# One order of rows to the end of layer 0, own terms kept on the chip, one scratch tile for the dots

## The chip, the cores and the metric

The kernel runs on one core of one Trainium2 chip. A core has five engines that work side by side, each on its own list of instructions: TensorE (PE, matrix products and transposes, with weight loads shown apart as PEld), VectorE (DVE), ScalarE (ACT), GpSimd (POOL, here almost only the issue of indirect transfers) and SyncE (SP, which issues transfers). An engine goes through its list in order and waits at an instruction until the semaphores that it names have their values. Transfers run on 16 DMA engines. The metric is the time of one execution on the device, in microseconds (us).

## The reference

Two graph layers over 2048 nodes, for 8 batches of 256 channels. The adjacency matrix is symmetric, has ones on its diagonal and about 1 in 128 entries set, so a node has some 11 to 36 neighbours.

```python
# layer 0
h1, h2, h3 = inp @ W1, inp @ W2, inp @ W3
e = leaky_relu(einsum('bnd,bmd->bnm', h1, h2), 0.2)
attention = softmax(where(adj > 0, e, -1e12))
x = layernorm(x + relu(einsum('bnm,bmd->bnd', attention, h3)))
# layer 1, 4 heads of 64
q = x @ W
e = leaky_relu(e_src[:, i] + e_dst[:, j], 0.2)     # q times the halves of a, per head
attn = softmax(where(adj > 0, e, -9e15))
x = layernorm(x + elu(einsum('bijh,bjhd->bihd', attn, q)))
```

## The kernel before

The kernel doesn't form the 2048 x 2048 scores. It sorts the nodes by degree, lists each node's neighbours, and fetches for each node the rows of its neighbours. The nodes stand in 16 tiles of 128 by degree; a tile has so many slots as its largest degree asks (SLOTS, 11 to 36). The batches are taken in two halves h of four (HB), so a row is 4 x 256 numbers (HC = 1024). A unit is one tile of one half in one layer: 32 units of layer 0, then 32 of layer 1, each with 11 to 27 slots, 564 slots in a layer.

A unit of layer 0 goes like this. POOL gathers the rows of the unit's own nodes (own_rows) and, slot by slot, those of their neighbours into a ring of 16 chunks of two slots (chunk_job; L203 is the helper that records all gathers). The own rows are transposed on PE (turn, L501), copied to xT by ACT, multiplied by A = W1 W2^T (project, L509) and copied to g. For each slot DVE makes four dots, one per batch (dots, L727): a product of the neighbour's row with g, written to a scratch tile j in bf16 that nothing reads, and behind it the read of the accumulator into the score e. Softmax follows (L768 to L779 on DVE, the exponential on ACT, weights0 from L838 on DVE). ACT makes a diagonal matrix of each slot's weights and batch (dg, L937), and PE adds the weighted rows up (add_slot, L901).

These sums use TensorE in four quarters of 64 x 64: row half r and column half c. So a sum stands in *quarter order*: partition 64c + n holds node 64r + n, and the batch pair is c. ACT or DVE brings it into hs, still in quarter order. Then after0: PE transposes hs (turn_h), ACT copies it to hT, PE multiplies by W3 (project_h), DVE adds relu of it to the own rows xr and collects the statistics (residual, L1055 and L1058), ACT normalises in place (L487), SP stores the rows to x1s in DRAM (L1080), PE transposes again (turn_x) and makes q and the head terms (queries, L1096), ACT copies them to q_rows (L1435 is the line that runs every delayed step), SP writes the four query-side terms per batch to own_d in DRAM (L1112), and POOL scatters the rows of q to the table qg by node number (L211). All of this was in quarter order, so before0 first puts the own rows into quarter order with four transfers from SBUF to SBUF (L704; by ACT's queue for the first two units, SP's for the others), and q is scattered in two halves, with the index orderP.

A unit of layer 1 loads its own terms from own_d (before1, L1140) and x1s (sums1, L1291), gathers rows of qg, adds own and neighbour's terms (L1163), does softmax, weights the rows on DVE and ACT (L984, L974) and adds them up on PE (L901).

The order of DVE, ACT, PE and POOL is written out by the program. A counter steps once a slot (tick): due(n, step) records a step n ticks later, and the dots run ahead of the sums by the next part's slots plus 9. The list of every engine is thus fixed. A tile pool with bufs=n hands out n buffers in turn, and a writer waits for the last user of its buffer, on its own engine too. The own rows have one buffer, xo_rows; a unit's gather is recorded once the unit before is transposed (turned). The ring, xo_rows and q_rows:

```python
g_rows = held[0][:, : 2 * HC].rearrange("p (i c) -> p i c", i=2)
xo_rows, hs_rows = held[1][:, :HC], held[1][:, HC : 2 * HC]
```

Of the kernel before, what the change touches and what calls it, by code (L numbers as in the profile page):

```python
# [13 lines left out]
F32 = mybir.dt.float32  # L14
BF16 = mybir.dt.bfloat16
# [9 lines left out]
P = 128  # L25
# [114 lines left out]
def fast_path(  # L140
# [82 lines left out]
    own_d = [tc.dram_tile([N, HG], F32, name=f"own_{h}") for h in range(2)]  # L223
# [7 lines left out]
    q_rows = held[2][:, 2 * KC * C :][:, : 2 * (QW + 2 * H)].rearrange("p (r w) -> p r w", r=2)  # L231
# [43 lines left out]
    spare = q_rows.rearrange("p r w -> p (r w)")  # L275
# [126 lines left out]
    orderP = const.tile([P, NT, 2], I32, tag="orderP", name="orderP")  # L402
    half = const.tile([P, NT, 2], F32, tag="half", name="half")
    oidx = const.tile([P, 2, 2, NT, 2], I32, tag="oidx", name="oidx")
# [19 lines left out]
    nc.vector.scalar_tensor_tensor(orderP, orderR, 2.0, half, ALU.mult, ALU.add)  # L424
# [106 lines left out]
    class Unit:  # L531
        def __init__(self, layer, h, t):
# [22 lines left out]
            self.xo = None  # L555
            self.ready = self.turned = False
# [41 lines left out]
    def neighbours(t):  # L598
# [30 lines left out]
        far = sp.tile([P, 40], F32, tag="far", name=f"far_{t}", bufs=2)[:, :K]  # L629
# [62 lines left out]
    def own_rows(u):  # L692
        u.xo = xo_rows
        gather(u.xo, xg[u.h][:, :], order[:, u.t : u.t + 1])

    def before0(u):
        while u.xo is None:
            yield
        xo = u.xo
        u.xr = xrp.tile([P, 2, HW], F32, tag="xr", name=f"xr_{u.name}")  # L700
        queue = nc.scalar if u.index < 2 else nc.sync
        for r in range(2):
            for c in range(2):
                queue.dma_start(  # L704
                    u.xr[64 * c : 64 * c + 64, r, :], xo[64 * r : 64 * r + 64, ts(c, HW)]
                )
# [3 lines left out]
        turn(xo, f"x_{u.name}", xT)  # L710
        u.turned = True
# [12 lines left out]
    def dots(u, rows, others, into):  # L724
        for b in range(HB):
            jt = sp.tile([P, C], BF16, tag="j", name=f"j_{u.name}_{clock[0]}_{b}", bufs=4)
# [304 lines left out]
    def after0(u):  # L1031
# [12 lines left out]
        def turn_h():  # L1044
            u.hT = wide_tile(f"hT_{n}")
            turn(u.hs, f"h_{n}", u.hT)
# [7 lines left out]
        def residual(i, pp):  # L1054
            nc.vector.scalar_tensor_tensor(  # L1055
                u.y[:, ts(i, 512)], pp, 0.0, u.xr[:, i, :], ALU.max, ALU.add
# [32 lines left out]
        def queries(r):  # L1089
            if r == 0:  # L1090
                u.qrow = q_rows
            for j in range(2):
                i = 2 * r + j
                pq = ps_tile(f"ps_q_{n}_{i}")
                for k in range(KC):
                    nc.tensor.matmul(  # L1096
                        pq[:, : C + 2 * H],
# [8 lines left out]
            if r == 1:  # L1106
                due(3, own_terms)
# [678 lines left out]
```

## Time and profile before

| | |
|---|---|
| median of three runs (lowest, highest) | 2446.78 us (2442.81, 2447.77) |
| the profiled execution | 2466.09 us, its span 2464.2 us |
| PE, DVE, ACT, POOL busy in the span | 84%, 79%, 57%, 59% |
| transfers | 734.65 MB, 298 GB/s on average |
| first and last dot of layer 0 | 105.9 and 1382.7 us |
| mean of a dot's product, of its accumulator read | 421 ns, 82 ns |
| sums on PE, layer 0 and layer 1 | 712.1 us, 826.8 us |

A line of a group reads: line, engine, operation, what it writes <- what it reads, shapes, number; then busy time in all, mean of one in ns; then how long the engine sat idle just before these, and what ended most of that. The busy times of a stretch give for each engine the time it worked, with the number of its instructions; PEclk is the clock that TensorE was granted, as a share of its full one. In the order of time a row has the start, the length, the instruction and, in brackets, the idle time before it with its releaser.

### The profile page before, as it was taken

What the parts mean: (1) busy time and instruction counts of PE and PEld (TensorE: products, weight loads), DVE (VectorE), ACT (ScalarE), POOL (GpSimd) and SP (SyncE); (2) the same over time, 40 slices, a digit from 0 to 9 for tenths busy, and PEclk for the clock granted to TensorE, in tenths of its full rate; (3) what the DMA queues carried; (4) which work ended last, traced back from release to release, by engine and by line L of the source; (5) the groups of instructions that cost most, each with busy time, mean ns of one, the idle gap of its engine ahead of it and who ended that gap; (6) DMA issues with size and microseconds to landing.
All of it is one profiled execution on the core that took longest, in us unless ns stands there. A gap on an engine that the chain in (4) does not pass through costs nothing.

```text
span 2464.2 us, 50609 instructions
## 1 busy us (share of the span) xinstructions
PE 2060.1 (84%) x16234; PEld 1097.8 (45%) x16234; DVE 1951.7 (79%) x6799; ACT 1403.6 (57%) x4803; POOL 1442.0 (59%) x1411
## 2 busy tenths in 40 slices
PE   4168898898888999999999888888788888788885
PEld 2135565555655666666656543333233233232221
DVE  7487688888888786788788568888877787787887
ACT  6045676566576677766677656443564555443545
POOL 3354555555555556555565566666666666666662
PEclk9578899999899999999999998888898888988888
DMA  9987898888877889898888898988998898889981
GB/s 377 360 272 267 291 306 313 294 306 273 296 260 253 300 286 310 286 303 290 288 278 293 272 341 318 317 311 315 329 331 311 306 343 298 322 311 327 326 300 46
DMA packets 239649, 734.65 MB, mean 298 GB/s; under 512 B 53456, under 2 KB 62800, under 8 KB 236944
## 3 DMA queue, kind: packets, MB, share of 16 engines
q0 software_dynamic: 182784, 645.78, 75.3%
q1 hardware_dynamic: 54720, 83.39, 10.1%
q8 instruction: 132, 2.16, 0.3%
q10 hardware_dynamic: 1872, 2.16, 0.3%
q14 instruction: 141, 1.16, 0.1%
HBM read 674.46 MB, written 76.02 MB: 305 GB/s over the span
## 4 chain that ended last, share of the span: by engine, by line
PE 48%; DVE 14%; issue 14%; ACT 8%; DMA 5%; another core or an unknown queue 4%; POOL 3%; SPq 0%; ACTq 0%; POOLq 0%; DVEq 0%
PE acc L901 32%; DVE s L984 6%; PE ps_q L1096 5%; PE ps_p_h L509 4%; PE ps_p_g L509 3%; POOL s L203 3%; ACT s L974 2%; DVE j L727 2%; DMA s<-qg,idx 2%; PE ps_t_x L501 2%; ACT dg L937 2%; PE ps_t_h L501 1%; DMA edges<-adj 1%; DVE xr L1339 1%
## 5 line engine op out<-in xcount | busy, mean ns | idle before, releaser
L901 PE MATMUL acc<-s,ident 64*64 64x512 f32 x4496 | 826.8, 673 | 165.7 <-issue 128.2
L203 POOL DMA_INDIRECT s<-xg,idx x564 | 591.1, 1048 | 512.8 <-PE acc L901 271.3
L727 DVE CUSTOM_DVE_ANT_0 j<-s,held 128x256 bf16<-128x256 f32 x2248 | 799.2, 421 | 58.5 <-ACT held L718 24.5
L901 PE MATMUL acc<-s,dg 64*64 64x256 f32 x8992 | 712.1, 401 | 113.4 <-issue 69.1
L203 POOL DMA_INDIRECT s<-qg,idx x564 | 573.0, 1016 | 299.9 <-issue 150.8
L937 ACT ACTIVATE dg<-twice,e 128x64 f32<-128x64 f32 x2248 | 574.0, 340 | 99.1 <-remote 60.2
L901 PEld LDWEIGHTS acc<-s,ident 64*64 64x64 f32 x4496 | 291.3, 148 | 689.2 <-issue 612.8
L901 PEld LDWEIGHTS acc<-s,dg 64*64 64x64 f32 x8992 | 395.3, 138 | 383.5 <-issue 203.7
L984 DVE TENSOR_TENSOR s<-s,p 128x2048 f32<-128x2048 f32 (+1 forms) x246 | 542.9, 2210 | 0.1
L974 ACT ACTIVATE s<-s,e 128x64 f32<-128x64 f32 x1376 | 342.7, 335 | 69.9 <-DVE e L1239 37.5
L727 DVE DVE_READ_ACCUMULATOR2_ANT e<- 128x1 f32 x2248 | 184.6, 82 | 0.4 <-issue 0.3
L211 POOL DMA_INDIRECT out_dram<-o,oidx x128 | 130.1, 1016 | 72.2 <-ACT o L487 36.0
L1435 ACT ACTIVATE e<-e 128x40 f32<-128x40 f32 (+19 forms) x88 | 27.5, 312 | 216.8 <-DVE e L1219 108.7
L1096 PE MATMUL ps_q<-wqs,x1T 128*128 128x264 f32 x512 | 135.8, 405 | 6.1 <-issue 3.5
L509 PE MATMUL ps_p_g<-held,xT 128*128 128x256 f32 x512 | 129.3, 407 | 13.4 <-ACT xT L1435 11.5
L509 PE MATMUL ps_p_h<-held,hT 128*128 128x256 f32 x512 | 120.0, 386 | 0.6 <-issue 0.6
L509 PEld LDWEIGHTS ps_p_g<-held,xT 128*128 128x128 f32 x512 | 101.6, 204 | 40.5 <-issue 13.1
L1096 PEld LDWEIGHTS ps_q<-wqs,x1T 128*128 128x128 f32 x512 | 93.8, 193 | 46.8 <-issue 21.5
L1055 DVE SCALAR_TENSOR_TENSOR y<-ps_p_h,xr 128x512 f32<-128x512 f32 x64 | 44.0, 688 | 85.5 <-PE ps_p_h L509 52.6
L1435 ACT COPY held<-ps_q 128x264 f32<-128x264 f32 x128 | 46.3, 379 | 110.8 <-PE ps_q L1096 93.6
L509 PEld LDWEIGHTS ps_p_h<-held,hT 128*128 128x128 f32 x512 | 94.8, 190 | 26.6 <-issue 14.3
L1163 DVE TENSOR_TENSOR e<-s,own 128x32 f32<-128x32 f32 (+1 forms) x290 | 53.0, 187 | 66.9 <-DMA s<-qg,idx 55.0
(206 smaller groups left out, 1549.9 us busy)
## 6 DMA issues: line engine op xcount, KB each, us to landing
adj<-in_adj_dram SPq DMA_DIRECT2D x16, 1024.0 KB
x1s<-y SPq DMA_DIRECT2D x32, 512.0 KB
xr<-x1s SPq DMA_DIRECT2D x32, 512.0 KB
xr<-held SPq DMA_DIRECT2D x120, 128.0 KB
s<-xg,idx POOLq DMA_INDIRECT x564
s<-qg,idx POOLq DMA_INDIRECT x564
edges<-adj SPq DMA_DIRECT2D x16, 512.0 KB
xg<-in_x_dram SPq DMA_DIRECT2D x4, 2048.0 KB
```

The source lines that it names most:

```text
L203: nc.gpsimd.indirect_dma_start(out=dst, out_offset=None, in_=table, in_offset=AT(ap=index, axis=0), bounds_check=table.shape[0] - 1, oob_i ...
L211: ins = nc.gpsimd.indirect_dma_start(out=table, out_offset=AT(ap=index, axis=0), in_=src, in_offset=None)
L501: nc.tensor.transpose(pt[:, ts(j, P)], src[:, ts(4 * i + j, P)], ident)
L509: nc.tensor.matmul(pp[:, ts(j, C)], lhsT=srcT[:, ts((2 * i + j) * KC + k, P)], rhs=weight[:, k, :], start=(k == 0), stop=(k == KC - 1),)
L727: nc.vector.tensor_tensor_reduce(out=jt, in0=rows[:, ts(b, C)], in1=others(b), scale=1.0, scalar=0.0, op0=ALU.mult, op1=ALU.add, accum_out ...
L901: nc.tensor.matmul(out, lhsT=lhsT, rhs=rhs, start=(k == 0 and j == 0), stop=(k == K - 1 and (j == 1 or diag is None)), tile_position=(64 * ...
L937: nc.scalar.activation(diag[:, b, :], twice, AF.Copy, scale=u.p[i][:, b, k : k + 1])
L974: nc.scalar.activation(v[:, a, g, :], v[:, a, g, :], AF.Copy, scale=pv[:, a, g : g + 1])
L984: nc.vector.tensor_tensor(v, v, pv.unsqueeze(3).to_broadcast([P, n, H, D]), ALU.mult)
L1096: nc.tensor.matmul(pq[:, : C + 2 * H], lhsT=u.x1T[:, ts(i * KC + k, P)], rhs=w.sqs[:, k, j * H : j * H + CD + H], start=(k == 0), stop=(k ...
L1163: nc.vector.tensor_tensor(e[:, k : k + ns, :].rearrange("p s (b g) -> p s b g", b=HB), rows[:, :ns, :].rearrange("p s (b w) -> p s b w", b ...
L1435: heappop(events)[2]()
```

## The change

Rows of layer 0 are brought into node order where hs is transposed, and stay in it: the copy from the transposes to hT puts the columns of the quarters next to each other (by_node), so that the projection, the residual, the normalisation, x1s and q have a node per partition. The own rows are gathered straight into the buffers xr, of which there are five (four of the pool, and xo_rows for every fifth unit), and serve the transposes and the residual; the transfers of L704 go, and a unit's gather is recorded once the buffer of the unit five before is free. q is scattered as whole rows with the index order. The four query-side terms per batch are copied by ACT into owns, a tile in SBUF that layer 1 reads; own_d, its stores and its loads go, and queries uses one set of columns, 260 in place of 264. x1s is in node order now, and layer 1 brings it into quarter order with four transfers in place of one. The scratch tile j of the dots has one buffer in place of four, and far, a small tile of the lists, one in place of two.

```diff
@@ -220,7 +220,6 @@
     edges = tc.dram_tile([N, N], I16, name="edges")
     x1s = [tc.dram_tile([N, HC], F32, name=f"x1s_{h}") for h in range(2)]
     qg = [tc.dram_tile([N, 2 * QW], F32, name=f"qg_{h}") for h in range(2)]
-    own_d = [tc.dram_tile([N, HG], F32, name=f"own_{h}") for h in range(2)]
 
 
     nc.scalar.preload_act_table_set("natural_log_exp_and_others")
@@ -228,7 +227,7 @@
     setup.__enter__()
     held = [ring_tile(f"held_{i}") for i in range(MORE)]
     kept = held[2][:, : 2 * KC * C].rearrange("p (i k c) -> p i k c", i=2, k=KC)
-    q_rows = held[2][:, 2 * KC * C :][:, : 2 * (QW + 2 * H)].rearrange("p (r w) -> p r w", r=2)
+    q_rows = held[2][:, 2 * KC * C :][:, : 2 * QW + 4 * H]
     w = Weights(nc, const, wp, ps_tile, w1, w2, w3, wq, a, C, "", (kept[:, 0], kept[:, 1]))
     ident = w.ident
 
@@ -399,8 +398,8 @@
 
 
     orderR = const.tile([P, NT, 2], I32, tag="orderR", name="orderR")
-    orderP = const.tile([P, NT, 2], I32, tag="orderP", name="orderP")
     half = const.tile([P, NT, 2], F32, tag="half", name="half")
+    owns = const.tile([P, 2, NT, HG], F32, tag="owns", name="owns")
     oidx = const.tile([P, 2, 2, NT, 2], I32, tag="oidx", name="oidx")
     idx = const.tile([P, total], I32, tag="idx", name="idx")
     neg = const.tile([P, total], F32, tag="neg", name="neg")
@@ -421,7 +420,6 @@
                 tile_position=(64 * r, 64 * c),
             )
         nc.vector.tensor_copy(orderR[:, :, r], pr)
-    nc.vector.scalar_tensor_tensor(orderP, orderR, 2.0, half, ALU.mult, ALU.add)
     w.terms()
     setup.__exit__(None, None, None)
     ctx.enter_context(tc.manual_schedule(engines={mybir.EngineType.Pool}))
@@ -552,8 +550,8 @@
             self.ps = [None] * len(self.parts)
 
             self.m, self.s, self.diags = [], [], []
-            self.xo = None
-            self.ready = self.turned = False
+            self.xr = None
+            self.ready = False
 
 
     scored, tabled = [0], [0]
@@ -626,7 +624,7 @@
                 nc.vector.match_replace(some, m[:, ts(i, 8)], some, 0.0)
             yield
         nc.vector.tensor_scalar(neg[:, o : o + K], m[:, :K], 0.5, LOWEST, ALU.is_lt, ALU.mult)
-        far = sp.tile([P, 40], F32, tag="far", name=f"far_{t}", bufs=2)[:, :K]
+        far = sp.tile([P, 40], F32, tag="far", name=f"far_{t}", bufs=1)[:, :K]
         nc.vector.tensor_scalar(far, m[:, :K], 0.5, FAR, ALU.is_lt, ALU.mult)
         nc.vector.scalar_tensor_tensor(
             idx[:, o : o + K], m[:, :K], 1.0, far, ALU.subtract, ALU.add
@@ -690,25 +688,19 @@
         numbered_extras[0] = True
 
     def own_rows(u):
-        u.xo = xo_rows
-        gather(u.xo, xg[u.h][:, :], order[:, u.t : u.t + 1])
+        if u.index % 5 == 3:
+            u.xr = xo_rows
+        else:
+            u.xr = xrp.tile([P, HC], F32, tag="xr", name=f"xr_{u.name}")
+        gather(u.xr, xg[u.h][:, :], order[:, u.t : u.t + 1])
 
     def before0(u):
-        while u.xo is None:
+        while u.xr is None:
             yield
-        xo = u.xo
-        u.xr = xrp.tile([P, 2, HW], F32, tag="xr", name=f"xr_{u.name}")
-        queue = nc.scalar if u.index < 2 else nc.sync
-        for r in range(2):
-            for c in range(2):
-                queue.dma_start(
-                    u.xr[64 * c : 64 * c + 64, r, :], xo[64 * r : 64 * r + 64, ts(c, HW)]
-                )
         for _ in range(4):
             yield
         xT = wide_tile(f"xT_{u.name}")
-        turn(xo, f"x_{u.name}", xT)
-        u.turned = True
+        turn(u.xr, f"x_{u.name}", xT)
         for _ in range(4):
             yield
         while scored[0] < u.index - 1:
@@ -723,7 +715,7 @@
 
     def dots(u, rows, others, into):
         for b in range(HB):
-            jt = sp.tile([P, C], BF16, tag="j", name=f"j_{u.name}_{clock[0]}_{b}", bufs=4)
+            jt = sp.tile([P, C], BF16, tag="j", name=f"j_{u.name}_{clock[0]}_{b}", bufs=1)
             nc.vector.tensor_tensor_reduce(
                 out=jt,
                 in0=rows[:, ts(b, C)],
@@ -1043,7 +1035,14 @@
 
         def turn_h():
             u.hT = wide_tile(f"hT_{n}")
-            turn(u.hs, f"h_{n}", u.hT)
+            by_node = u.hT[:, :HC].rearrange("p (c j k r n) -> p j (k r) c n", c=2, j=2, k=KC, r=2)
+            for j in range(2):
+                pt = ps_tile(f"ps_t_h_{n}_{j}")
+                for k in range(KC):
+                    for r in range(2):
+                        o = r * HW + j * C + k * P
+                        nc.tensor.transpose(pt[:, ts(2 * k + r, P)], u.hs[:, o : o + P], ident)
+                due(2, nc.scalar.copy, by_node[:, j], pt.rearrange("p (a c n) -> p a c n", a=4, c=2))
 
         def project_h():
             u.y = wide_tile(f"y0_{n}")[:, :HC]
@@ -1053,7 +1052,7 @@
 
         def residual(i, pp):
             nc.vector.scalar_tensor_tensor(
-                u.y[:, ts(i, 512)], pp, 0.0, u.xr[:, i, :], ALU.max, ALU.add
+                u.y[:, ts(i, 512)], pp, 0.0, u.xr[:, ts(i, 512)], ALU.max, ALU.add
             )
             nc.vector.bn_stats(
                 u.st[:, i, :], u.yb[:, 2 * i : 2 * i + 2, :].rearrange("p b c -> p c b")
@@ -1087,42 +1086,24 @@
             due(6, queries, 1)
 
         def queries(r):
-            if r == 0:
-                u.qrow = q_rows
-            for j in range(2):
-                i = 2 * r + j
-                pq = ps_tile(f"ps_q_{n}_{i}")
+            u.qrow = q_rows
+            for b in range(2 * r, 2 * r + 2):
+                pq = ps_tile(f"ps_q_{n}_{b}")
                 for k in range(KC):
                     nc.tensor.matmul(
-                        pq[:, : C + 2 * H],
-                        lhsT=u.x1T[:, ts(i * KC + k, P)],
-                        rhs=w.sqs[:, k, j * H : j * H + CD + H],
+                        pq[:, : CD + H],
+                        lhsT=u.x1T[:, ts(b * KC + k, P)],
+                        rhs=w.wqs[:, k, :],
                         start=(k == 0),
                         stop=(k == KC - 1),
                     )
-                due(
-                    2, nc.scalar.copy, u.qrow[:, r, ts(j, CD + H)], pq[:, : CD + H]
-                )
+                due(2, nc.scalar.copy, u.qrow[:, ts(b, CD)], pq[:, :CD])
+                due(2, nc.scalar.copy, owns[:, h, t, ts(b, H)], pq[:, CD : CD + H])
             if r == 1:
-                due(3, own_terms)
-
-        def own_terms():
-            for c in range(2):
-                for j in range(2):
-                    nc.sync.dma_start(
-                        own_d[h][ts(t, P), ts(2 * c + j, H)].rearrange("(r p) g -> p r g", r=2),
-                        u.qrow[64 * c : 64 * c + 64, :, j * (QW + H) : j * (QW + H) + H],
-                    )
-            late.append((clock[0] + 1, store))
+                due(3, lambda: late.append((clock[0] + 1, store)))
 
         def store():
-            for r in range(2):
-                scatter(
-                    f"q{h}",
-                    qg[h].rearrange("n (q c) -> (n q) c", q=2),
-                    orderP[:, t, r : r + 1],
-                    u.qrow[:, r, H : H + QW],
-                )
+            scatter(f"q{h}", qg[h][:, :], order[:, t : t + 1], u.qrow[:, : HB * CD])
             tabled[0] += 1
             if tabled[0] == 2 * NT:
                 credits[0] += MORE
@@ -1136,8 +1117,7 @@
 
     def before1(u):
         h, t = u.h, u.t
-        u.own = sp.tile([P, HG], F32, tag="own", name=f"own_{u.name}")
-        nc.sync.dma_start(u.own, own_d[h][ts(t, P), :])
+        u.own = owns[:, h, t, :]
         u.ready = True
         yield
 
@@ -1288,7 +1268,12 @@
 
     def sums1(u):
         u.xr = xrp.tile([P, 2, HW], F32, tag="xr", name=f"xr_{u.name}")
-        nc.sync.dma_start(u.xr.rearrange("p r c -> p (r c)"), x1s[u.h][ts(u.t, P), :])
+        for r in range(2):
+            for c in range(2):
+                nc.sync.dma_start(
+                    u.xr[64 * c : 64 * c + 64, r, :],
+                    x1s[u.h][u.t * P + 64 * r : u.t * P + 64 * r + 64, ts(c, HW)],
+                )
         u.accs = []
         for i, part in enumerate(u.parts):
             acc = None
@@ -1424,8 +1409,9 @@
 
     def tick(limit):
         m = owned[0]
-        free = m < 5 and (m != 1 or len(units[0].chunks[0]) > 2) or m - 5 in rested and clock[0] >= rested[m - 5] + 4
-        if m < min(opened[0] + 4, 2 * NT) and free and (m == 0 or units[m - 1].turned):
+        free = m < 4 or m == 4 and listed[up[2]]
+        free = free or m - 5 in rested and clock[0] >= rested[m - 5] + 4
+        if m < min(opened[0] + 4, 2 * NT) and free:
             own_rows(units[m])
             owned[0] += 1
         pump()
```

More of the change, by code (lines that the diff above doesn't have):

```diff
@@ L274, in fast_path @@
     homes = rest[:, 7 * P :][:, : 3 * NT * NT].rearrange("p (t f s) -> p t f s", t=NT, f=3)
-    spare = q_rows.rearrange("p r w -> p (r w)")
+    spare = q_rows
     row, down = (spare[:, ts(i, P)] for i in range(2))
```

## The prediction

> **What bounds the kernel now.** I read the busy times of two stretches first, because the two layers have different limits: layer 0 from the first dot to the last (106 to 1383 us) and layer 1 (1400 to 2400 us).
>
> ```profile
> core 0: us, PE busy (x) PEld busy (x) DVE busy (x) ACT busy (x) POOL busy (x), PEclk, DMA share, GB/s
> 106.00:1383.00 1277.00, 1134.86 (x11034) 745.12 (x11032) 1053.47 (x5544) 825.38 (x2917) 700.34 (x667) 0.94 0.86 288
> 1400.00:2400.00 1000.00, 838.46 (x4640) 311.44 (x4638) 785.37 (x1078) 492.23 (x1697) 676.32 (x665) 0.86 0.90 318
> ```
>
> In layer 0 PE is busy 89% and sets the pace; DVE has 82%, DMA 86%, ACT 65%, POOL 55%. Layer 1 is paced by the transfers (90%), PE (84%) and DVE (79%) together. Second, the groups of DVE in 106:1383, for what fills it and where it waits:
>
> ```profile
> L727 DVE CUSTOM_DVE_ANT_0 j<-s,held 128x256 bf16<-128x256 f32 x2248 | 799.2, 421 | 58.5 <-ACT held L718 24.5 <-DMA s<-xg,idx 24.3 <-issue 5.0
> L727 DVE DVE_READ_ACCUMULATOR2_ANT e<- 128x1 f32 x2247 | 184.5, 82 | 0.4 <-issue 0.3
> L1055 DVE SCALAR_TENSOR_TENSOR y<-ps_p_h,xr 128x512 f32<-128x512 f32 x60 | 41.3, 688 | 81.1 <-PE ps_p_h L509 52.6 <-issue 15.0 <-remote 13.6
> L839 DVE TENSOR_REDUCE s<-e 128x4 f32<-128x40 f32 (+8 forms) x53 | 10.4, 197 | 39.5 <-ACT e L1435 26.1 <-ACT dg L937 10.6 <-ACT held L1435 1.5
> L477 DVE SCALAR_TENSOR_TENSOR rstd<-z 128x4 f32<-128x4 f32 x30 | 4.9, 163 | 17.3 <-ACT z L470 11.8 <-ACT dg L937 5.0 <-issue 0.2
> ```
>
> The dots fill DVE. Its idle time is 1277.0 - 1053.5 = 223.5 us: about 19 us are gaps of 34 ns between operations that need each other's result (each of those groups shows 1 to 2.5 us), and 204 us are waits for late partners, mostly PE (81.1 before the residual) and ACT. That is all the slack DVE has. Third, the order of time on DVE, 128 to 129.5 us, which decides this case:
>
> ```profile
> 127.84 0.41 DVE L727 CUSTOM_DVE_ANT_0 j<-s,held 128x256 bf16<-128x256 f32 x1
> 128.18 0.08 DVE L727 DVE_READ_ACCUMULATOR2_ANT e<- 128x1 f32 x1
> 128.18 0.41 DVE L727 CUSTOM_DVE_ANT_0 j<-s,held 128x256 bf16<-128x256 f32 x1
> 128.53 0.08 DVE L727 DVE_READ_ACCUMULATOR2_ANT e<- 128x1 f32 x1
> 128.53 0.41 DVE L727 CUSTOM_DVE_ANT_0 j<-s,held 128x256 bf16<-128x256 f32 x1
> 128.87 0.08 DVE L727 DVE_READ_ACCUMULATOR2_ANT e<- 128x1 f32 x1
> 128.99 0.20 DVE L768 SCALAR_TENSOR_TENSOR e<-e 128x44 f32<-128x44 f32 x1
> ```
>
> A dot is a pair, the product and the read of its accumulator. The next product starts with that read, 0.346 us after its predecessor (127.84, 128.18, 128.53), while the predecessor still has 0.07 us to run. L768 needs what the read writes and waits for it: it starts at 128.99, 0.46 us after the last product. Over layer 0 the median is 346 ns for the 2013 products that directly follow a dot, and 465 ns (456 to 475) for the 36 times that L768 does. So waiting for the read in front costs 119 ns.
>
> **The change part by part.** (1) *One scratch tile for the dots.* The four tiles of before make a product wait for the dot four back, long done: in the built program 1484 products wait for something seven or more instructions back, 772 for nothing. With one tile, the second write must follow the first, and in the changed program as built 2013 of 2256 products wait for the accumulator read directly in front of them. No result is shared, but the wait is the one that L768 shows. Behind a waiting product stand all later dots, the residual and the weights on DVE; ACT's diagonals wait for the weights, PE's sums for the diagonals. Price: 2013 x 0.119 = 239.5 us of DVE in layer 0. DVE then needs 1053.5 + 239.5 + 19 = 1312 us where the stretch has 1277: with every one of the 204 us of waits gone it is 35 us longer; with every one kept, 239.5 us. PE needs 1135 us plus 63 us that its sums show as idle with no releaser, 1198 in all, so it falls behind DVE as the limit. The waits for PE and ACT shrink, since those get slack, but don't all go. In the stretch before, PE as the limit took 1198 of 1277 us: 79 us, 6%, went to partners. After the change DVE needs 9% more than PE (1312 to 1198); before, PE needed 12% more than DVE (1198 to 1072). The two cases are alike, so a like loss is due, a bit less because the largest wait, the residual's 81.1 us, had PE itself as its cause: I take 60 us, between the 0 and 204 of the two ends. Layer 0: 35 + 60 = +95 us.
>
> A rule of the Trainium skill speaks against this step. "VectorE: DVE Perf Modes", section "The DRAIN you can't avoid", says that chained Vector operations pay the flush of the pipeline anyway and that a semaphore after each costs nothing extra, by eight copies that took 13.88 us both ways; by it the pitch would stay and the whole sum would be about -2 us. The trace differs, with 346 ns against 465 ns behind the same read, and I go by the trace.
>
> (2) *Start of layer 0.* Before, ACT issues the eight transfers xr<-held of the first two units, and POOL waits for the one buffer of own rows:
>
> ```profile
> 90.01 10.70 ACTq L704 DMA_DIRECT2D xr<-held  x4
> 100.81 1.07 ACT L1435 COPY xT<-ps_t_x 128x512 f32<-128x512 f32 x2 [42.47 <-DMA edges<-adj]
> 105.89 0.42 DVE L727 CUSTOM_DVE_ANT_0 j<-s,held 128x256 bf16<-128x256 f32 x1 [19.54 <-ACT held L718]
> 125.38 0.99 POOL L203 DMA_INDIRECT held<-xg,order  x1 [9.57 <-DVE e L727]
> ```
>
> The transposes of unit 0 end at 92.0, but xT is copied at 100.8. Without the transfers the copies end near 93, and g's first half can be there at 98. But POOL now issues three more gathers of own rows (units 1 to 3) ahead of the first neighbours: their issue moves from 87.2 by 3 x 1.30 us to 91.1, and with the 8.5 us that the own rows took (issued 81.57, transposed at 90.08) they land at 99.6. First dot 99.6 in place of 105.9: -6 us. Bounds: 0, if 1.5 MB more on a DMA that is full here adds 5 us, and -12, if the 9.6 us of POOL's stall at 115 to 125 go as well. I take -6.
>
> (3) *Transfers that go.* The 128 xr<-held (8192 packets of 2048 bytes, 116 ns each in the trace's packet records: 59 us of 16 engines), the 128 stores of own terms (16384 packets of 16 bytes, 9 ns: 9 us), and 32 of 64 scatters (1.065 us each on POOL). All lie where DMA has 86% and POOL 55%, beside an engine that is the limit: 0, bounded by 0 and -68. SP's queue loses 280 issues and nothing waits behind it for compute but the x1s stores. POOL's later own-row gathers stand at the same slots as before relative to the transposes that need them (9 to 18 slots ahead), so none is newly late.
>
> (4) *Added on ACT:* 128 copies of 128x4. Nearest row: f<-ps_f, 128x2, 160 ns; 20.5 us, beside DVE's limit in an ACT that idles a third. The strided hT copies: row 585 ns x 64; equal or, at worst, doubled, +37 us of ACT. Both at nothing; the cover is ACT's idle 450 us, and without it they would cost 20 to 58 us. The single buffer of far was last read a whole neighbour list earlier: 0. PE's ps_q matmuls are 4 of 264 columns narrower: -2 us, hidden.
>
> (5) *Layer 1:* x1s is loaded by four transfers of 64 rows with 2 KB runs for one with 4 KB; same bytes, 96 more issues on SP, 32 own-term loads less. The packets of 4096 bytes took 188 ns in layer 1 (4096 of them, 48 us of 16 engines); 8192 halves at layer 0's 116 ns are 59 us, and the 64-byte loads that go had 3 us: +8 us of DMA time, or -3 if halves cost half. DMA has 90% here, so I let half of it show: +4. The own terms' waits on DVE showed no DMA of their own: 0.
>
> Sum: 95 - 6 + 0 + 0 + 4 = +93 us. The profiled execution took 2466.09 us (span 2464.2 and 1.9 around), 19.3 us over the median 2446.78; 2466.1 + 93 - 19.3 = 2540 us.
>
> **The rivals.** A, *the wait is free* (not slower): at the products, the read has posted before the next product could start, and the pitch stays 0.346. For it: products already wait on the same counter at no visible cost; against it: those waits are old, and the 36 cases of L768 all took 456 ns or more. The turning point is a rise of about (204 - 60)/2013 = 0.07 us per dot: below it DVE's idle time swallows it. Then -6 + 4 and up to a seventh of the 68 us of DMA time: 2435 to 2447.
>
> B, *DVE absorbs it*: the pitch rises, but PE and ACT get so far ahead that nearly no wait is left: +35 to +60 in layer 0, 2480 to 2503. For it: 81 of the 204 us are waits for a PE that then has slack. Against: the exponentials (39.5) and roots (17.3) are round trips between DVE and ACT that stay in the written order.
>
> C, *the waits stay*: the order of DVE, ACT and PE is fixed slot by slot, so a slower DVE delays PE and the residual waits as long as before; +150 to +239 us, 2595 to 2684. Against it: over the 564 slots of the layer DVE then gives PE 2.33 us for each (1312/564), and PE needs 2.12 (1198/564), so it stops being late.
>
> **How the numbers follow.** Forecast (layer 0 +60 to +150): 0.65, 2540 us. B 0.17, C 0.10, A 0.08 (0.05 under the bound of 0.2%, which is 5 us, 0.03 within it). Slower: 0.92. The range leaves out A and most of C: 2480 to 2612; the forecast's own is 2503 to 2595.
>
> **What would show it.** Right: the median distance of two products near 0.46 us, products' idle gaps of 34 ns summing up on L727, DVE above 90% in layer 0 and PE near 80%, the residual's 81 us shrunk, the first dot near 100 us, layer 1 within 10 us of its 1000. Wrong: a pitch of 0.346; or a pitch of 0.46 with PE still the limit, which would say that the 204 us were real slack; or layer 1 moving by more than 15 us.

## The result, and the profile after

The changed kernel takes 2512.22 us (median of four executions, 2510.22 to 2516.59) against 2446.93 us for the kernel before (four, 2442.81 to 2447.77): a ratio of 1.0273, with a 95% interval of 1.0255 to 1.0291, or +65 us. The forecast was 2540 us, +93 us. The profiled execution of after took 2513.24 us (span 2511.0), which is its median within 1 us, while the profiled one of before was 19.3 us over its median. So the two traces differ by 47 us where the kernels differ by 65, and lengths of stretches of before are those of a somewhat slow execution.

The experiments below ran on other chips, and the chips differ: on all of those but one pair's the kernel before takes 2193 us in place of 2447. So each experiment is compared with the kernel before on its own chip, and the two kernels of this case were run there again.

First, the busy times of the two stretches of after, in the columns that the prediction's first fence names (length of the stretch, then PE, PEld, DVE, ACT, POOL, the granted clock, the DMA share and GB/s). Layer 0 is taken from its first dot to its last:

```profile
107.00:1443.70 1336.70, 1106.78 (x11060) 727.80 (x11060) 1219.45 (x5546) 833.38 (x3041) 673.88 (x639) 0.92 0.77 263
1460.00:2450.00 990.00, 801.35 (x4629) 300.98 (x4625) 787.72 (x1080) 493.95 (x1705) 672.04 (x662) 0.85 0.92 320
```

Layer 0 lasts 1336.7 us where it lasted 1277: +59 us by the two traces. DVE is busy for 1219 us, 166 more than before, and has 91% of the stretch where it had 82%; PE went from 89% to 83%, DMA from 86% to 77%. The limit has changed engines. Layer 1 has the same rates as before within a few per cent.

Second, the groups of DVE in the same stretch (busy time in all, mean of one in ns, idle time just before them and what ended it):

```profile
L719 DVE CUSTOM_DVE_ANT_0 j<-s,held 128x256 bf16<-128x256 f32 x2248 | 954.2, 424 | 98.1 <-DMA s<-xg,idx 25.9 <-ACT held L710 1.3 <-DVE e L719 0.8
L719 DVE DVE_READ_ACCUMULATOR2_ANT e<- 128x1 f32 x2248 | 183.7, 82 | 0.0
...
L1054 DVE SCALAR_TENSOR_TENSOR y<-ps_p_h,xr 128x512 f32<-128x512 f32 x48 | 32.9, 685 | 16.5 <-PE ps_p_h L507 16.5
...
L831 DVE TENSOR_REDUCE s<-e 128x4 f32<-128x40 f32 (+8 forms) x53 | 10.3, 194 | 2.5 <-ACT e L1421 1.7
...
L1054 DVE SCALAR_TENSOR_TENSOR y<-ps_p_h,held 128x512 f32<-128x512 f32 x12 | 8.2, 686 | 2.6 <-PE ps_p_h L507 2.6
...
L475 DVE SCALAR_TENSOR_TENSOR rstd<-z 128x4 f32<-128x4 f32 x30 | 4.7, 158 | 0.0
```

A product itself is no longer than before (424 ns to 421), but its group has 155 us more of busy time, because a product no longer starts while the one in front is still running. And 98.1 us of idle time stand before the products: 28.0 have a releaser, the other 70 are gaps of 34 ns between instructions of DVE itself. The waits for partners have almost gone: the residual's 81.1 us are 16.5 + 2.6 = 19.1 (the twelve rows with held are the units whose own rows lie in xo_rows), the weights' 39.5 are 2.5, the root's 17.3 are 0.

Third, DVE in the order of time (start, length, instruction):

```profile
132.84 0.42 DVE L719 CUSTOM_DVE_ANT_0 j<-s,held 128x256 bf16<-128x256 f32 x1
133.19 0.08 DVE L719 DVE_READ_ACCUMULATOR2_ANT e<- 128x1 f32 x1
133.31 0.42 DVE L719 CUSTOM_DVE_ANT_0 j<-s,held 128x256 bf16<-128x256 f32 x1
133.66 0.08 DVE L719 DVE_READ_ACCUMULATOR2_ANT e<- 128x1 f32 x1
133.78 0.42 DVE L719 CUSTOM_DVE_ANT_0 j<-s,held 128x256 bf16<-128x256 f32 x1
```

Before, a product started with the read in front of it. Now the read runs from 133.19 to 133.27, and the product starts 34 ns behind it, at 133.31. The distance of two products is 467 ns over the layer (median), 346 before. In before, L768 had shown 465 ns for the same wait.

Fourth, the sums on PE in layer 0 of after, in the same columns as the groups of DVE:

```profile
L893 PE MATMUL acc<-s,dg 64*64 64x256 f32 x8688 | 652.3, 403 | 130.7 <-ACT dg L929 83.9 <-issue 26.0 <-ACT e L1421 12.6
```

PE now waits 83.9 us for ACT's diagonals; before it was 33.6 us. ACT in turn waits 84.8 us for DVE's scores ahead of the exponential, in place of 18.3. The engines behind DVE now wait for it.

Fifth, the start, from the order of time of POOL, ACT and DVE (in brackets the idle time before, with its releaser):

```profile
88.42 0.99 POOL L203 DMA_INDIRECT held<-xg,order  x1 [0.30 <-issue]
89.71 0.99 POOL L203 DMA_INDIRECT s<-xg,idx  x1 [0.30 <-issue]
...
95.42 0.58 ACT L710 COPY held<-ps_p_g 128x512 f32<-128x512 f32 x1 [1.47 <-PE ps_p_g L507]
...
107.01 0.43 DVE L719 CUSTOM_DVE_ANT_0 j<-s,held 128x256 bf16<-128x256 f32 x1 [20.88 <-DMA s<-xg,idx]
```

g is ready at 96 (first half), but the first dot doesn't start before 107.0: it waits for the neighbours' rows, issued 17.3 us before, at 89.71, behind the own rows of three later units.

### The profile page after: what moved, and what is told of

Read it like the earlier page. It is cut to its first block, busy times and chain, and to the rows that moved or that the text cites. A ratio compares the mean times of both kernels' runs of the same rounds, so it can differ in the third digit from the quotient of the medians.

```text
span 2511.0 us, 50307 instructions
## 1 busy us (share of the span) xinstructions
PE 1999.2 (80%) x16234; PEld 1072.9 (43%) x16234; DVE 2117.5 (84%) x6798; ACT 1412.2 (56%) x4931; POOL 1410.6 (56%) x1379
## 5 line engine op out<-in xcount | busy, mean ns | idle before, releaser
L719 DVE CUSTOM_DVE_ANT_0 j<-s,held 128x256 bf16<-128x256 f32 x2248 | 954.2, 424 | 98.1 <-DMA s<-xg,idx 25.9
L203 POOL DMA_INDIRECT s<-xg,idx x564 | 594.0, 1053 | 635.1 <-PE acc L893 326.6
L893 PE MATMUL acc<-s,ident 64*64 64x512 f32 x4496 | 796.5, 682 | 189.3 <-issue 150.8
L893 PE MATMUL acc<-s,dg 64*64 64x256 f32 x8992 | 676.5, 402 | 135.7 <-ACT dg L929 83.9
L893 PEld LDWEIGHTS acc<-s,dg 64*64 64x64 f32 x8992 | 373.9, 139 | 393.3 <-ACT dg L929 138.5
L1093 PE MATMUL ps_q<-wqs,x1T 128*128 128x264 f32 x512 | 141.1, 418 | 33.0 <-DVE y L1054 22.1
L507 PE MATMUL ps_p_g<-held,xT 128*128 128x256 f32 x512 | 122.6, 394 | 19.7 <-ACT xT L1421 17.4
L1421 ACT COPY held<-ps_q 128x260 f32<-128x260 f32 x128 | 47.1, 377 | 125.3 <-PE ps_q L1093 84.4
L507 PEld LDWEIGHTS ps_p_g<-held,xT 128*128 128x128 f32 x512 | 97.5, 195 | 43.3 <-ACT xT L1421 17.8
L1143 DVE TENSOR_TENSOR e<-s,owns 128x32 f32<-128x32 f32 (+1 forms) x290 | 52.7, 186 | 71.8 <-DMA s<-qg,idx 60.1
L1321 DVE TENSOR_TENSOR xr<-xr,ex 128x1024 f32<-128x1024 f32 x32 | 39.2, 1225 | 75.5 <-ACT ex L1318 48.0
```

The costliest lines, as they stand in the source:

```text
L203: nc.gpsimd.indirect_dma_start(out=dst, out_offset=None, in_=table, in_offset=AT(ap=index, axis=0), bounds_check=table.shape[0] - 1, oob_i ...
L507: nc.tensor.matmul(pp[:, ts(j, C)], lhsT=srcT[:, ts((2 * i + j) * KC + k, P)], rhs=weight[:, k, :], start=(k == 0), stop=(k == KC - 1),)
L719: nc.vector.tensor_tensor_reduce(out=jt, in0=rows[:, ts(b, C)], in1=others(b), scale=1.0, scalar=0.0, op0=ALU.mult, op1=ALU.add, accum_out ...
L893: nc.tensor.matmul(out, lhsT=lhsT, rhs=rhs, start=(k == 0 and j == 0), stop=(k == K - 1 and (j == 1 or diag is None)), tile_position=(64 * ...
L1093: nc.tensor.matmul(pq[:, : CD + H], lhsT=u.x1T[:, ts(b * KC + k, P)], rhs=w.wqs[:, k, :], start=(k == 0), stop=(k == KC - 1),)
L1143: nc.vector.tensor_tensor(e[:, k : k + ns, :].rearrange("p s (b g) -> p s b g", b=HB), rows[:, :ns, :].rearrange("p s (b w) -> p s b w", b ...
```

## The experiments

Two things were open. Is the product's wait the whole loss, or does the rest of the change (the order of rows, own rows, layer 1's four loads) take a part? And by what rule do some 240 us more of DVE's time become 59 us? My theory for the second: layer 0 lasts about as long as the slower of DVE and PE needs, so the wait costs nothing while PE is the slower and its full price from then on. The rivals are a loss in proportion to the number of waits, and one that comes from elsewhere. Lengths of layer 0 are from the first to the last dot, those of layer 1 from there to the end, each from the profiled execution of the kernel.

### The two kernels again, on a chip of the experiments

> The kernel before, unchanged, for a profile on the chip of the experiments, where it takes 2193 us and not 2447. Theory P (PE's sums go faster there, DVE's work is the same): layer 0 takes 1120 to 1135 us from first to last dot, DVE busy 1045 to 1055 us in it, layer 1 from the last dot to the end 950 to 960 us. Rival D (DVE or the transfers are faster there): DVE's dots shorter than 421 ns, or its busy time below 1030 us.

> The changed kernel, unchanged, on the chip of the experiments. Theory W (layer 0 is DVE's need of 1312 us and some 25 us of waits on any chip, since PE is not the limit): 1330 to 1340 us from first to last dot as on the first chip, 2395 to 2412 us in all. The kernel with one tile and nothing else took 2393 us, with layer 1 in 952 us; four loads of x1s add about 11 us to layer 1. Rival R (the loss scales with the chip, 2.7% as on the first): about 2253 us.

| us | first dot | layer 0 | layer 1 | time, or ratio to before |
|---|---|---|---|---|
| before, first chip | 105.9 | 1277.2 | 1081.1 | 2446.93 |
| after, first chip | 107.0 | 1336.6 | 1067.4 | 1.0273 (1.0255 to 1.0291) |
| before, second chip | 105.6 | 1128.7 | 954.8 | 2191.0 (one execution; median of nine there 2193.01) |
| after, second chip | 106.9 | 1329.8 | 960.0 | 1.0921 (1.0905 to 1.0938), 2396.89 |

The same change costs 65 us on one chip and 204 us on another. After's layer 0 is the same on both, 1337 and 1330 us. Before's isn't: 1277 and 1129. Busy times of before's layer 0 on the second chip:

```profile
105.60:1234.30 1128.70, 1018.26 (x11067) 693.45 (x11069) 1047.29 (x5546) 818.80 (x2925) 705.78 (x667) 0.95 0.93 326
```

DVE does the same work there (1047 us to 1053), but has 93% of the stretch: on this chip DVE was the limit before the change already. What differs is PE. The sums of layer 0 on the first chip, and then on the second, in before's groups of PE:

```profile
L901 PE MATMUL acc<-s,dg 64*64 64x256 f32 x8656 | 684.2, 400 | 107.5 <-issue 63.4 <-ACT dg L937 33.6 <-ACT x1T L1435 1.5
```

```profile
L901 PE MATMUL acc<-s,dg 64*64 64x256 f32 x8676 | 573.5, 392 | 63.3 <-ACT dg L937 62.8 <-issue 0.2
```

One matmul takes as long on both (400 and 392 ns), but the same sums fill 684 us on the first chip and 574 on the second, and the 63 us of idle time without a releaser are on the first alone. The 1198 us of PE on which the prediction rests thus belong to the chip that they were read on, and in part to that execution: in after on the first chip the same sums have 26.0 us of such idle time, not 63.4. Before came out as expected, and after with the loss in full; a loss that scales with the kernel's time (2.7% again) is out.

### One scratch tile alone

```diff
-            jt = sp.tile([P, C], BF16, tag="j", name=f"j_{u.name}_{clock[0]}_{b}", bufs=4)
+            jt = sp.tile([P, C], BF16, tag="j", name=f"j_{u.name}_{clock[0]}_{b}", bufs=1)
```

The kernel before, with this edit and nothing else. It ran on two chips.

> The kernel before with one change: the scratch tile of the dots has one buffer in place of four. Theory W (the wait for the accumulator read in front is the whole loss, all other parts of the change sum to about nothing): median distance of two products 0.467 us, DVE needs about 1312 us for layer 0 plus some 25 us of waits, 1337 us from first to last dot; time 2505 to 2515 us, as the changed kernel. Rival G (the other parts gain and hide a larger loss): above 2520 us. Rival C (the other parts cost a share): 2460 to 2500 us.

> The kernel before with one scratch tile and nothing else, once more, since its first run was on a chip where the kernel before takes 2193 us. On a chip where the kernel before takes 2445 us, theory M (DVE's need of 1312 us and some 22 us of waits, beside a layer 0 of 1277): 2497 to 2512 us, as the changed kernel's 2512 less the 5 us of its other parts. On a chip of 2193 us: 2388 to 2397 us again.

Measured: 2392.57 us, ratio 1.0901 (1.0880 to 1.0921), and 2393.59 us, 1.0915 (1.0897 to 1.0934). The time expected of the first run was that of the first chip and is missed for that reason; the length of layer 0 was met, as its busy times show, and behind them those of after on the second chip:

```profile
105.70:1439.10 1333.40, 1078.32 (x11075) 721.38 (x11073) 1219.22 (x5546) 821.71 (x2925) 710.51 (x669) 0.90 0.81 277
```

```profile
106.90:1436.70 1329.80, 1072.92 (x11060) 716.23 (x11060) 1218.46 (x5546) 828.03 (x3041) 680.55 (x639) 0.91 0.75 264
```

DVE is busy for 1219.22 us, to 1218.46 in after, and layer 0 takes 1333 and 1330 us in the two runs, to 1330 in after. One line makes nearly the whole loss: +199 us of the +204. The rest of the change adds 3 to 4 us net on these chips, and the intervals overlap. On a chip like the first this edit was not run alone. That it makes the loss there too is argued: after has the same pitch, the same busy time of DVE and within 7 us the same layer 0 on both kinds of chip, but how the 65 us are shared out between the tile and the rest is not shown.

### All of the change but the single scratch tile

The changed kernel with two scratch tiles. Their space comes from narrower work tiles, and far takes the place of a tile that has been read.

```diff
-        return wp.tile([P, 2 * QW], F32, tag="t", name=name)
+        return wp.tile([P, HC], F32, tag="t", name=name)
...
-        far = sp.tile([P, 40], F32, tag="far", name=f"far_{t}", bufs=1)[:, :K]
+        far = some[:, :K]
...
-            jt = sp.tile([P, C], BF16, tag="j", name=f"j_{u.name}_{clock[0]}_{b}", bufs=1)
+            jt = sp.tile([P, C], BF16, tag="j", name=f"j_{u.name}_{clock[0]}_{b}", bufs=2)
```

> The changed kernel with two scratch tiles for the dots; the room comes from wide tiles of 1024 in place of 1040 numbers and from the tile far, which goes into a dead part of the tile some. A product then waits for the read two dots back. Theory W: median distance 0.346 us, DVE about 82% busy in layer 0 again, 2440 to 2452 us. Rival G: below 2435 us. Rival C: 2455 us or more.

Measured: 2179.89 us, ratio 0.9937 (0.9924 to 0.9951). The busy times of layer 0:

```profile
107.30:1218.70 1111.40, 1004.23 (x11060) 685.10 (x11060) 1046.31 (x5546) 824.11 (x3041) 674.28 (x637) 0.97 0.88 315
```

Two tiles are enough: DVE is busy for 1046.3 us again, and the distance of two products is 346 ns. Without the wait the rest of the change is a small gain of 13 us, which none of the expectations, written for the first chip, gives in size. Layer 0 is 17 us shorter (1111.4 us), layer 1 is 2 us longer (956.8), and the first dot comes at 107.3.

Most of the 17 us are gained early: dot 188 of the 2256 comes 97.5 us after the first in place of 106.4, dot 376 207.8 in place of 222.0. What POOL does there, in before on the second chip, and then in this kernel:

```profile
124.93 0.99 POOL L203 DMA_INDIRECT held<-xg,order  x1 [11.06 <-DVE e L727]
```

```profile
124.56 1.05 POOL L203 DMA_INDIRECT s<-xg,idx  x1 [9.94 <-DVE e L719]
```

Before, the first gather after POOL's stall is that of own rows, and the neighbours' rows come behind it; in the changed kernel own rows have been fetched, and neighbours come first. DVE's waits for neighbours' rows fall from 25.9 us to 9.6 behind the first dot. That the one makes the other was not tried by itself. POOL's stall itself, which the bound of -12 in the prediction's step 2 let go, is nearly as long as before (9.9 us to 11.1). With the single tile the early gain is gone: dot 376 comes 245 us after the first in after on the second chip and 247 with one scratch tile alone. A slower DVE has less need to wait for those rows.

### Half of the waits

Before, with two pairs of dots on a tile each, so that every second product waits for the read in front of it: 1128 in place of 2013.

```diff
-            jt = sp.tile([P, C], BF16, tag="j", name=f"j_{u.name}_{clock[0]}_{b}", bufs=4)
+            jt = sp.tile([P, C], BF16, tag=f"j{b // 2}", name=f"j_{u.name}_{clock[0]}_{b}", bufs=1)
```

> The kernel before, with one scratch tile for the dots of batches 0 and 1 and one for 2 and 3, so that every second product waits for the read in front of it. DVE needs 1072 + 1128 x 0.119 = 1206 us in layer 0, PE 1198 us. Theory K (two engines near the limit lose to each other, as the 6% of PE before): 1277 us grow to 1290 to 1310, 2460 to 2480 us. Rival S (the 204 us of waits swallow whatever stays under them, and only DVE's need above 1277 us shows): within 5 us of before, 2442 to 2452 us.

Measured: 2296.58 us, ratio 1.0465 (1.0446 to 1.0484). The products in the order of time:

```profile
149.85 0.42 DVE L727 CUSTOM_DVE_ANT_0 j<-s,held 128x256 bf16<-128x256 f32 x1
...
150.20 0.42 DVE L727 CUSTOM_DVE_ANT_0 j<-s,held 128x256 bf16<-128x256 f32 x1
...
150.66 0.42 DVE L727 CUSTOM_DVE_ANT_0 j<-s,held 128x256 bf16<-128x256 f32 x1
...
151.01 0.42 DVE L727 CUSTOM_DVE_ANT_0 j<-s,held 128x256 bf16<-128x256 f32 x1
```

The distances alternate, 0.35 and 0.46 us, so each wait has the price by itself. 1128 x 0.119 = 134 us of DVE made layer 0 110 us longer (1238.5 to 1128.7). Both theories had expected less, for a chip on which DVE had 204 us of waits to lose; here it had some 62. So this run says nothing on where the price begins, which was its question. It does show that the loss goes by the number of waits once DVE is the limit: 56% of the waits cost 55% of the 201 us.

### More work on PE

If layer 0 goes by the slower engine, the single tile must cost nothing where PE is slower still. Both kernels, with the projections to g and h made twice over (the second writes over the first, 4 matmuls more of 128x256 for each product of 512 columns):

```diff
-            for j in range(2):
+            for j in (0, 1, 0, 1):
```

> The kernel before, with PE's matmuls of both projections of layer 0 made twice, the second time over the first, so that the result is the same: 64 x 3.65 = 234 us more of PE in layer 0, to give PE about the load that it had on the first chip. Theory M (what the wait of the dots costs is what it adds beyond the slower of DVE and PE): layer 0 goes from 1129 us to 1255 to 1330, in all 2320 to 2400 us.

> The changed kernel with the same doubled projections. Theory M: DVE's 1312 us are still the larger need, layer 0 stays at 1330 to 1360 us, 2395 to 2430 us in all, and the distance to the kernel before with doubled projections is 30 to 100 us in place of 204. Rival R (the wait costs its 205 us on this chip whatever PE does, as the two add up): 2520 us or more.

The pair ran on a chip like the first (before 2444.87 us), not like those that its expectations were written for. Measured: before with more PE 2589.73 us (1.0582 of before, 1.0547 to 1.0617), after with more PE 2584.33 (1.0561, 1.0524 to 1.0598). Busy times of layer 0 of the one, and then of the other:

```profile
106.90:1508.40 1401.50, 1294.22 (x12025) 906.18 (x12024) 1057.26 (x5546) 830.55 (x2923) 695.87 (x667) 0.97 0.78 262
```

```profile
106.90:1509.10 1402.20, 1288.24 (x12036) 899.90 (x12036) 1222.65 (x5546) 833.38 (x3041) 670.93 (x639) 0.96 0.73 251
```

DVE has its 165 us of busy time more here too, and layer 0 is as long: 1401.5 and 1402.2 us. The wait is there and costs nothing. DVE's idle time fell from 344.2 to 179.6 us, by as much as its work grew. The largest part of that is in the waits of DVE for the residual's partner (us, times, longest), first before with more PE, then after:

```profile
DVE y L1055 <- PE ps_p_h L509: 136.6, 47, 17.0
```

```profile
DVE y L1054 <- PE ps_p_h L507: 52.2, 28, 13.9
```

A slower DVE waits less for the same PE. A difference of 30 to 100 us had been expected between the two kernels; it is -5.4 us. So the rule of the slower engine holds on both sides: +201 us where DVE was the limit already, +59 us where PE was a little slower, 0 where PE was much slower. A loss by the number of waits alone is out, since all 2013 are there in each of the three. Near the balance the rule gives no size: by the needs alone the first chip would have lost 110 us (1308, worked out below, less 1198), and it lost 59 because the limit had 79 us of waits beside it before and 29 after.

### Layer 1's four loads alone

Before, with x1s loaded by four transfers of 64 rows and 2 KB runs. The rows keep the order they have there.

```diff
-        nc.sync.dma_start(u.xr.rearrange("p r c -> p (r c)"), x1s[u.h][ts(u.t, P), :])
+        for r in range(2):
+            for c in range(2):
+                nc.sync.dma_start(
+                    u.xr[64 * c : 64 * c + 64, r, :],
+                    x1s[u.h][u.t * P + 64 * c : u.t * P + 64 * c + 64, ts(r, HW)],
+                )
```

> The kernel before, with each load of x1s in layer 1 made as four of 64 rows with runs of 2 KB, with the same result. Theory of step 5: +4 us (-3 to +8) of a layer where transfers have 90%; 2447 to 2455 us. Rival: the loads are hidden and nothing shows, 2444 to 2449 us.

Measured: 2204.58 us, ratio 1.0051 (1.0033 to 1.0070), or +11 us; layer 1 goes from 954.8 to 965.6. The busy times from 1250 to 2150 us, in before on the second chip, and then here:

```profile
1250.00:2150.00 900.00, 632.30 (x4716) 201.17 (x4708) 805.18 (x1105) 498.21 (x1726) 682.22 (x672) 0.88 0.95 355
```

```profile
1250.00:2150.00 900.00, 630.71 (x4684) 201.37 (x4676) 797.40 (x1097) 490.94 (x1705) 682.11 (x670) 0.87 0.99 355
```

The same 355 GB/s keep the DMA engines busy for 99% in place of 95%, and every other engine does a little less. The step's +4 (bound +8) was too low for a chip on which layer 1 is limited by the transfers.

### The start, and the order at the store

Two edits on top of the changed kernel with two tiles. The first holds back the own rows of units 1 to 3 until the first unit's first neighbours are issued, which is the rule of before:

```diff
-        free = m < 4 or m == 4 and listed[up[2]]
+        free = m < 4 and (m != 1 or len(units[0].chunks[0]) > 2) or m == 4 and listed[up[2]]
```

> The changed kernel with two scratch tiles, and with the gathers of the own rows of units 1 to 3 behind the first three chunks of unit 0's neighbours. Theory of step 2 as the profile after corrects it (g is there at 97 us, the first dots wait for the neighbours' rows until 107 us): the first dot comes at 100 to 103 us, 4 to 7 us below the kernel with two tiles alone, 2173 to 2177 us. Rival (the transfers of the edges, which fill the queues to 108 us, end the wait): first dot at 106 to 108 us, 2178 to 2184 us.

Measured: 2176.16 us, ratio 0.9914 (0.9900 to 0.9927). The first dot:

```profile
100.53 0.43 DVE L719 CUSTOM_DVE_ANT_0 j<-s,held 128x256 bf16<-128x256 f32 x1 [15.56 <-DMA s<-xg,idx]
```

It comes at 100.5 in place of 107.3: the three gathers ahead had held up the first neighbours. Of these 6.8 us some 4 to 5 reach the end, by the two ratios, whose intervals overlap a little; layer 0 is 3 us longer (1114.3).

The second leaves that and brings x1s into quarter order at the store, in layer 0, so that layer 1 loads it with one transfer again:

```diff
-                nc.sync.dma_start(x1s[h][ts(t, P), :], u.y)
+                for r in range(2):
+                    for c in range(2):
+                        nc.sync.dma_start(
+                            x1s[h][t * P + 64 * c : t * P + 64 * c + 64, ts(r, HW)],
+                            u.y[64 * r : 64 * r + 64, ts(c, HW)],
+                        )
```

> The one before in this list, and x1s in quarter order again: four stores of 64 rows in layer 0 in place of one, one load in layer 1 in place of four. Theory (runs of 2 KB cost only where transfers are the limit, in layer 1): layer 1 shorter by 8 to 13 us, layer 0 longer by 0 to 4 us, 2164 to 2172 us. Rival (the cost moves to layer 0 with the stores): within 3 us of the one before.

> The changed kernel with two scratch tiles, the gathers of units 1 to 3 behind the first chunks, and x1s in quarter order, once more. On a chip where the kernel before takes 2445 us, PE is the limit of layer 0, and what the other parts save (transfers, POOL's stall at the start) lies mostly beside it: 2425 to 2442 us. On a chip of 2193 us: 2163 to 2169 us again.

Measured: 2165.88 us, ratio 0.9874 (0.9859 to 0.9889), and on another chip 2165.68, 0.9876 (0.9859 to 0.9892). Layer 1 falls from 961.5 to 950.8 and 950.4 us, layer 0 stays (1113.9 and 1113.1). So the four transfers cost 11 us in layer 1 and nothing that shows in layer 0, where the DMA share is 0.88. This version is faster than before and after: the change without its single tile, with its two small losses mended, gains 27 us, or 1.3%. No version with two tiles was run on a chip like the first.

## Why the prediction was right, and where a step failed

**The bound, and the wait (step 1).** Right in kind and in size. The distance of two products is 467 ns for 465 forecast, DVE alone needs 1336.7 us less the waits for partners, 29, or 1308 us, for 1312 forecast, and PE lost its place as the limit. One scratch tile alone reproduces the loss on the chips where it ran. The rule of the Trainium skill that was weighed against it ("VectorE: DVE Perf Modes", section "The DRAIN you can't avoid": in eight copies, a semaphore after each added nothing to the flush of the pipeline) can't be carried over to this pair of instructions: the same product starts 0.346 us after the one in front without the wait and 0.467 us with it.

**The waits that stay (in step 1).** This is the term that was mis-sized. I took 60 us, by the loss to partners that the stretch had before when PE was the limit (79 us). Measured are 29 us in after: of the 25.9 us for neighbours' rows 20.9 lie before the first dot, so 5.0 are left, 19.1 for the residual, and 5.0 for all others. The likeness of the two ratios (9% and 12%) was no argument: after the change DVE waits for hardly anyone, and it is PE that waits for DVE, by ACT's diagonals (83.9 us). Layer 0 is +59, not +95: 31 us of the 36 too much are this term, the other 4 the 1312. Step 2's miss took 7 back, and the forecast lay 28 us too high. The result lies between the range of rival B (2480 to 2503; its upper end is 2505 by its own sum, 60 - 6 + 4 us over 2446.8) and my middle. My argument against B, that the exponentials (39.5) and roots (17.3) are round trips that stay, was wrong: 2.5 and 0 are left.

**The start (step 2).** Wrong: 107.0 us, later by 1 us, where I had 99.6. The own rows, the transposes and g came earlier as worked out (g's first half at 96, forecast 98). The neighbours' rows were issued in time as well, at 89.71 for 91.1 forecast. The term that was wrong is their 8.5 us from issue to landing, taken from unit 0's own rows, which have no such gather ahead of them: the dot came 17.3 us after the issue. I counted the three gathers of own rows ahead as 1.30 us of POOL each. But gathers land one behind the other: by the semaphore updates in after's trace, the own rows of units 1 to 3 are complete at 100.1, 102.6 and 104.8 us and the first neighbours at 106.9. That is what the bound of 0 was for, and the result lies just beyond it. Holding the gathers back brought 100.5, still 14.7 us behind the issue (at 85.86). POOL's stall, which the bound of -12 let go, stays: 11.5 us in after.

**The transfers that go (3) and ACT's additions (4).** Nothing on the limit, as costed. One scratch tile alone, without any of it, has layer 0 at 1333 and 1330 us, the whole change at 1330. The strided copies to hT take 585 ns, as before. One small term was misread: the matmuls of queries (ps_q) did not become narrower. Both traces have them with 264 columns, and only ACT's copy of their result went from 264 to 260. The 2 us were counted as hidden, so the sum doesn't change.

**Layer 1 (step 5).** On the first chip the medians leave 65.3 - 59.4 - 1.1 = 4.8 us for all that is neither layer 0 nor its start, to +4 forecast. That hangs on where the profiled execution of before spent the 19 us over its median. Its layer 1 was 13.7 us longer than after's. On the second chip before's is 5 us shorter, but in the pair with more PE, on a chip like the first, it is 6 us longer (1077.6 to 1071.6). If layer 1 moved so on the first chip too, the change gained 6 us there and lost about 70 us in layer 0 at the median, not 59. So the +4 is not confirmed, and the loss in layer 0 is known as some 59 to 70 us. By itself the step cost 11 us on chips where layer 1 is faster, above the bound of +8.

**The rivals.** A fell with the pitch of 467 ns. C fell with the residual's 19.1 us. But C's price is what the other chips show, +201 us in layer 0, and by another way: not since the waits stayed, but since there were only some 62 us of them to lose. And A's result, no change, is what the pair with more PE shows, since DVE's idle time swallows the wait. The balance between PE and DVE decided which of these it was, and that balance differs between chips. That the time was met owes something to luck: kernel and profile were on the same chip, and on the second kind the forecast (a ratio of 1.038) would have missed the 1.0921 by far.

## What to carry to other kernels

A buffer that nobody reads is still a wait: with one of them every write waits for the last, and here two give back all that four gave. Price such a wait by the same pair of instructions elsewhere in the trace (0.346 to 0.465 us behind the same read), multiply, and then ask how far the engine is from being the limit: the same 240 us of its time cost 0, some 59 to 70, or 201 us. The waits beside the old limit are no measure for those beside the new one: here they were 79 us with PE as the limit and 29 with DVE, which makes the scores that ACT and PE wait for. And look at every input of the first instruction, not at the one that came last before, and count how long the transfers ahead of it take to land, not how long they take to issue.

## What the runs showed of the hardware that was not expected

Chips differ by more than the change. On one kind the kernel before takes 2445 to 2447 us, on the other 2193 to 2194, at a mean granted clock of 0.895 and 0.91. DVE's work is the same on both (1053 and 1047 us in layer 0), PE's isn't: in the whole span the sums of layer 0 fill 712.1 and 594.6 us, those of layer 1 826.8 and 610.6, though one matmul takes 401 and 392 ns, 673 and 685 ns. So by the records, in which the ends of matmuls are modelled, fewer of them are under way at once on the first kind (8992 x 0.401 / 712.1 = 5.1, to 5.9). The same working gives 5.1 to 5.4 in the four traces of the first kind and 5.8 to 6.0 in the ten of the second, and for layer 1's sums 3.7 to 3.9 and 5.0 to 5.1, so it goes with the kind of chip and not with the kernel. In layer 0 the sums of before have 69.1 us of idle time without a releaser on the first kind and 0.2 on the second. What holds PE's queue up there is open; no run here tells.
